# Edge rows of a graph layer: one queue fetches rows singly instead of three engines, and the gathered rows share one pool of eight buffers

## The chip, the cores and the metric

The kernel runs on one core of one Trainium2 chip. The metric is the device time of one execution in microseconds (us); the number quoted for a kernel is the median of its timed runs. The core has five engines with a queue of instructions each: TensorE (PE, with its weight loads shown as PEld), VectorE (DVE), ScalarE (ACT), GpSimd (POOL) and SyncE (SP). They meet only through semaphores, and 16 DMA engines move the data.

## The reference

A graph layer over N = 12500 nodes with 128 features and E = 400000 edges with 32 attributes; the edges come sorted by destination.

```python
h = jnp.maximum(_layernorm(x, axis=-1), 0.0)
# for every edge (s -> d):
m = relu(concat([h[s], h[d], ea]) @ w1 + b1) @ w2 + b2
agg = segment_sum(m, d, num_segments=12500)
# a GRU cell with input agg and state h gives h'
out = x + h'
```

The whole is float32. What costs is `h[s]`: 400000 rows of 512 bytes in random order.

## The kernel before, in words

A first stage normalises all nodes, keeps h transposed on chip (`hT_all`, 128 features by 12500 nodes), multiplies it by the first 128 rows of w1 and writes the product to a table `A` in device memory. After that an edge needs one row of `A` instead of a row of h and a product.

The edges are cut into 391 double groups of 1024 edges (eight tiles of 128; the first has five), numbered k. A double group is two units, u = 2k and 2k + 1, of four tiles each. The loop over u at the end of the kernel writes out the order of all work by hand; for a unit it issues, a few units ahead of each other:

- `pre(u+3)`: TensorE adds destination part and edge attributes into PSUM (L599);
- `add(u+2)`: VectorE adds the gathered rows of `A` in place (L624);
- `relu(u+2)`: ScalarE writes the result to a ring of three `RB` (L630); this is the last reader of the gathered rows;
- `seg(u)`: TensorE sums the edges of a destination with a one-hot matrix (L643), and `take` copies the sums out (L651, L652).

`window`, `onehot` and `onehot_T` prepare the matrices on VectorE. After every 14 double groups `node(b)` runs the GRU for a block of 512 nodes, spread over the units that follow.

The rows of `A` arrive in three ways.

**Gathers.** `gather(k)` issues eight indirect DMAs of 128 rows on GpSimd (L147) into a buffer `G` of 128 x 8 x 128 floats. The buffer is free once the relu of unit 2 x taker + 1 is done, where `taker[k]` is the double group that had it before. The pool `gp` has 7 buffers. Another pool `ge` of 4 buffers serves double groups 0 to 3 and 11 to 14 and is closed at unit 30. The first `RAW` = 10 double groups can't wait for `A`: they gather rows of x, and VectorE, ScalarE and TensorE normalise and turn them on the way (`raw_stats`, `raw_fin`, `raw_h`, `raw_turn`).

**Rows one by one (SyncE).** Six double groups are brought by SyncE: 1024 numbers of source nodes lie in one partition of a small tile `at`; 32 at a time are loaded into registers (L789), and one DMA per row (L802) copies 512 bytes of `A` into a buffer `G_sp` of its own. The queue of SyncE also brings the edge attributes `L` (L486) and the destinations `Ld` (L495) of every second double group, the node numbers (L103, L114), and the rows and results of a node block (L665, L734), in the order in which the loop issues them.

**Columns one by one (VectorE and ScalarE).** For 18 double groups VectorE, and for 19 ScalarE, copies a column of `hT_all` per edge, found by a register, into a tile of 128 x 1024 (L797, L795); `pre` then multiplies these columns by w1 on TensorE (L610), and there is nothing to add.

Which double group goes which way is fixed when the kernel is built (`SPREAD`). `run_jobs` spreads the single copies of a job evenly over the units between its start and its end, four times a unit: a job of SyncE begins two units after the last one's double group and is due 8 units before its own. `gathers(u)` issues each gather as soon as the relu that frees its buffer has been issued.

```python
def gathers(u):
    while asked[0] < NP and (asked[0] in mode or 2 * taker[asked[0]] + 1 < u + 2):
        gather(asked[0])
        asked[0] += 1
```

Of the kernel before, what the change touches and what calls it, by code (L numbers as in the profile page):

```python
# [20 lines left out]

GRP = 4
PAIR = 2 * GRP
SUP0 = T % PAIR
NP = T // PAIR + 1
# [11 lines left out]
NT = -(-N // 128)  # L37
NFULL = N // 128
BAT = (4,) + (8,) * 11 + (NFULL - 92, 1)
RAW = 10  # L40
GBUFS = 7
EARLY = 4
PLACE = 20
CH = PLACE * PAIR
LOAD = 32
STEP = {"act": 4, "dve": 4, "sp": 2}
SPREAD = {"dve": 18, "act": 19, "sp": 6}
NR = 12672

H_AT = 16512  # L50

ROW = 512
HOLD = -2


@with_exitstack
def tile_gnn(ctx: ExitStack, tc: tile.TileContext, x, src, srcT, dstT, dstP, eaT, eaP, w1, b1, w2T, b2,
             wih, bih, whh, bhh, out):
    nc = tc.nc
    ctx.enter_context(tc.manual_schedule())  # L60
    const = ctx.enter_context(tc.tile_pool(name="const", bufs=1))
    hT_all = const.tile([128, N], F32, name="hT_all")
    h_bytes = hT_all.bitcast(U8)
    gp = ctx.enter_context(tc.tile_pool(name="gp", bufs=GBUFS))
    p2 = ctx.enter_context(tc.tile_pool(name="p2", bufs=2))
    p3i = ctx.enter_context(tc.tile_pool(name="p3i", bufs=3))
    early = ExitStack()
    ge = early.enter_context(tc.tile_pool(name="ge", bufs=EARLY, side="right"))
    ps2 = ctx.enter_context(tc.tile_pool(name="ps2", bufs=2, space=bass.MemoryType.PSUM))
    ps1 = ctx.enter_context(tc.tile_pool(name="ps1", bufs=1, space=bass.MemoryType.PSUM))  # L70
    dram = ctx.enter_context(tc.tile_pool(name="dram", bufs=1, space=bass.MemoryType.DRAM))
# [8 lines left out]
        return [(t0 + a * GRP + j, j, a) for j in (2 * h, 2 * h + 1) for a in range(2)  # L80
                if t0 + a * GRP + j < t1]

    JOBS0 = 2 * EARLY + GBUFS

    mode, order = {}, {m: [] for m in SPREAD}
    for m, n in SPREAD.items():
        lo, hi = {"dve": (JOBS0 + 3, NP - 14), "act": (JOBS0 + 11, NP - 6),
                  "sp": (JOBS0 + 5, NP - 10)}[m]
        for i in range(n):
            k = lo + int((i + 1) * (hi - lo) / n)  # L90
            while k in mode:
                k += 1
            mode[k] = m
            order[m].append(k)


    src_i = {}
# [26 lines left out]

    G = {}

    def early_pair(k):
        return k < EARLY or EARLY + GBUFS <= k < 2 * EARLY + GBUFS

    taker, rings = {}, {True: [], False: []}  # L130
    for k in range(NP):
        if k not in mode:
            ring = rings[early_pair(k)]
            size = EARLY if early_pair(k) else GBUFS
            taker[k] = ring[-size] if len(ring) >= size else -1
            ring.append(k)

    def gather(k):
        if k >= NP or k in mode:
            return  # L140
        pool = ge if early_pair(k) else gp
        G[k] = pool.tile([128, GRP, 2, D], F32, name="G")
        table = x if k < RAW else A
        for u in (2 * k, 2 * k + 1):
            for t, j, a in unit_tiles(u):
                c, i = divmod(t, CH)
                nc.gpsimd.indirect_dma_start(  # L147
                    out=G[k][:, j, a, :], out_offset=None, in_=table,
                    in_offset=bass.IndirectOffsetOnAxis(ap=src_i[c][:, i:i + 1], axis=0))
# [61 lines left out]
    with tc.tile_pool(name="pp", bufs=3) as pp:  # L211
# [50 lines left out]
        rows = const.tile([1, 6 * D + D], F32, name="rows")  # L262
# [212 lines left out]


    Ls, Ds, OH, RT, HE, SEG = ({} for _ in range(6))
    hand = {}

    def fetch(q):  # L480
        if q * QP >= NP:
# [109 lines left out]
    def pre(u):  # L591
        if u >= NU:
            return
        k, h = divmod(u, 2)
        PP[u] = ps2.tile([128, GRP, D], F32, name="pre")
        for i in range(2):
            c0 = (k % QP) * 512 + (2 * h + i) * 128
            raw = u in HE or k in hand
            nc.tensor.matmul(PP[u][:, 2 * i:2 * i + 2, :], Ls[k // QP][:, c0:c0 + 128], RW[k % 4],  # L599
                             start=True, stop=not raw)  # L600
            if raw:
                l = unit_tiles(u)
                for n, (t, j, a) in enumerate(l):
                    if j % 2 == i:
                        if k in hand:
                            c = (a * GRP + j) * 128
                            cols = hand[k][:, c:c + 128]
                        else:
                            cols = HE[u][:, n * 128:(n + 1) * 128]
                        nc.tensor.matmul(PP[u][:, 2 * i + a, :], cols, w1a, start=False,  # L610
                                         stop=n + 1 == len(l) or l[n + 1][1] != j)


    def add(u):
        if u >= NU:
            return
        if u in HE or u // 2 in hand:
            RT[u] = PP.pop(u)
            HE.pop(u, None)
            if u % 2:  # L620
                hand.pop(u // 2, None)
        else:
            RT[u] = unit(u)
            nc.vector.tensor_tensor(RT[u], PP.pop(u), RT[u], op=ALU.add)  # L624
# [132 lines left out]
        return o  # L757


    pj = []  # L760
    late = ExitStack()
    by_hand = [k for m in ("sp", "act", "dve") for k in order[m]]
    NJ = len(by_hand)
    NSP = len(order["sp"])

    place_of = const.tile([NJ, 2], F32, name="place_of")
    for i, (to_sp, to_others) in enumerate(((ROW, 4), (0, H_AT))):
        nc.vector.memset(place_of[:, i:i + 1], float(to_others))
        nc.vector.memset(place_of[:NSP, i:i + 1], float(to_sp))
    A_bytes = A.bitcast(U8).rearrange("n f -> (n f)")  # L770
    at = const.tile([NJ, PAIR * 128], I32, name="at")

# [2 lines left out]
        nc.sync.dma_start(at[r:r + 1, :], src[t0 * 128:(t0 + PAIR) * 128].rearrange(  # L775
            "(o e) -> o e", o=1))

    def one_by_one(m, k):
        et = {"act": ET.Activation, "dve": ET.DVE, "sp": ET.SP}[m]
        r = by_hand.index(k)  # L780
        if m == "sp":
            G[k] = pj[0].tile([128, GRP, 2, D], F32, name="G_sp", bufs=1)
            rows = G[k].bitcast(U8)
        else:
            hand[k] = pj[0].tile([128, PAIR * 128], F32, name=f"HE_{m}")
            he = hand[k].bitcast(U8)
        for e0 in range(0, PAIR * 128, LOAD):
            low, high = (0, ROW * (N - 1)) if m == "sp" else (H_AT, H_AT + 4 * (N - 1))
            _, vals = nc.values_load_multi_w_load_instructions(  # L789
                at[r:r + 1, e0:e0 + LOAD], engines=[et], min_val=low, max_val=high,  # L790
                skip_runtime_bounds_check_because="src holds numbers of nodes")
            for i, v in enumerate(vals):
                e = e0 + i
                if m == "act":
                    nc.scalar.copy(he[:, e * 4:e * 4 + 4], h_bytes[:, bass.ds(v - H_AT, 4)])  # L795
                elif m == "dve":
                    nc.vector.tensor_reduce(he[:, e * 4:e * 4 + 4],  # L797
                                            h_bytes[:, bass.ds(v - H_AT, 4), None],
                                            AX.X, ALU.max)
                else:  # L800
                    a, j = divmod(e // 128, GRP)
                    nc.sync.dma_start(rows[e % 128:e % 128 + 1, j, a, :],  # L802
                                      A_bytes[bass.ds(v, ROW)].rearrange("(o f) -> o f", o=1))
                if i % STEP[m] == STEP[m] - 1:
                    yield


    jobs = {}
    for m, kl in order.items():
        start = 2 * JOBS0  # L810
        for k in kl:
            end = 2 * k - (8 if m == "sp" else 4)
            jobs.setdefault(start, []).append((m, k, end - start))
            start = end if m != "sp" else 2 * k + 2
    live = {}

    PH = 4

    def run_jobs(u, phase):
        if u == 2 * JOBS0 and phase == 0:  # L820
            early.close()
            pj.append(late.enter_context(tc.tile_pool(name="pj", bufs=2, side="right")))
        if phase == 0:
            for m, k, span in jobs.get(u, ()):
                live[m] = [one_by_one(m, k), u, span, PAIR * 128 // STEP[m], 0]
        for m, job in list(live.items()):
            it, start, span, steps, done = job
            want = -(-steps * ((u - start) * PH + phase + 1) // (span * PH))
            while job[4] < want:
                job[4] += 1  # L830
                if next(it, "end") == "end":
                    del live[m]
                    break


    asked = [RAW]

    def gathers(u):
        while asked[0] < NP and (asked[0] in mode or 2 * taker[asked[0]] + 1 < u + 2):
            gather(asked[0])  # L840
            asked[0] += 1

# [46 lines left out]
    for u in range(NU):  # L889
        k, h = divmod(u, 2)  # L890
        gathers(u)
        if h == 0:
# [9 lines left out]
                dst_tile(k // PLACE + 2)  # L902
            if k == NP - 20:
                check_windows()
        for r in range(2 * u, min(2 * u + 2, NJ)):
            job_indices(r)
        if u == 2 * JOBS0 - 2:
            nc.vector.tensor_scalar(at, at, place_of[:, 0:1], place_of[:, 1:2],
                                    op0=ALU.mult, op1=ALU.add)

        def other(phase):
            run_jobs(u, phase)
# [190 lines left out]
```

## Time and profile before

| what | before |
|---|---|
| median of 3 runs | 5420.59 us (5406.4 to 5431.38) |
| profiled execution | 5395.6 us, its span 5393.5 us |
| instructions | 95106 |
| busy share PE, DVE, ACT, POOL | 58%, 50%, 50%, 49% |
| gathers of rows of `A` (L147) | 2704, 955 ns each |
| column copies, ScalarE (L795) | 19456, 189 ns each |
| column copies, VectorE (L797) | 18432, 146 ns each |
| row DMAs of SyncE (L802) | 6144 of 0.5 KB |

The profile is one execution. A line of a view names the line of the kernel, the engine, the operation, what it writes and reads, and how often; "idle before" is the time for which the engine had nothing running just ahead of these instructions, and the name after the arrow is what ended most of it ("issue": nothing that the profile shows). Instructions that only load registers, branch or start a DMA are not counted as busy. Times within the run are us from its first instruction.

### The profile page before, as it was taken

What the parts mean: (1) busy time and instruction counts of PE and PEld (TensorE: products, weight loads), DVE (VectorE), ACT (ScalarE), POOL (GpSimd) and SP (SyncE); (2) the same over time, 40 slices, a digit from 0 to 9 for tenths busy, and PEclk for the clock granted to TensorE, in tenths of its full rate; (3) what the DMA queues carried; (4) which work ended last, traced back from release to release, by engine and by line L of the source; (5) the groups of instructions that cost most, each with busy time, mean ns of one, the idle gap of its engine ahead of it and who ended that gap; (6) DMA issues with size and microseconds to landing.
All of it is one profiled execution on the core that took longest, in us unless ns stands there. A gap on an engine that the chain in (4) does not pass through costs nothing. (4 is left out here: it accounts for less than half of the span.)

```text
span 5393.5 us, 95106 instructions
## 1 busy us (share of the span) xinstructions
PE 3101.8 (58%) x13578; PEld 1854.8 (34%) x13578; DVE 2712.7 (50%) x22515; ACT 2718.9 (50%) x20936; POOL 2654.9 (49%) x2789
## 2 busy tenths in 40 slices
PE   2664555556555556556655555665556565556557
PEld 2542333333333323333333333333333233333334
DVE  3645545545454545455545455545454555555453
ACT  2433345555555555555555555555555555555554
POOL 5445445544555454545454555544455544544452
PEclk7775665666566666666666666666666666666667
DMA  3322122222222222222221222222222222222221
GB/s 107 90 65 63 52 58 63 62 56 56 60 59 59 60 60 55 61 57 62 56 60 52 58 61 58 61 60 56 60 58 56 59 60 58 60 58 58 57 58 44
DMA packets 157887, 325.93 MB, mean 60 GB/s; under 512 B 65057, under 2 KB 77132, under 8 KB 157255
## 3 DMA queue, kind: packets, MB, share of 16 engines
q0 software_dynamic: 88992, 182.43, 13.1%
q1 hardware_dynamic: 68119, 137.33, 8.9%
q14 instruction: 520, 4.26, 0.3%
q8 instruction: 112, 1.84, 0.1%
q10 hardware_dynamic: 144, 0.07, 0.0%
HBM read 305.74 MB, written 13.84 MB: 59 GB/s over the span
## 5 line engine op out<-in xcount | busy, mean ns | idle before, releaser
L147 POOL DMA_INDIRECT G<-A,src_i x2704 | 2581.1, 955 | 2658.2 <-ACT RB L630 1766.9
L795 ACT COPY HE_act<-hT_all 128x4 uint8 x19456 | 2155.6, 189 | 1758.6 <-issue 1733.5
L797 DVE TENSOR_REDUCE HE_dve<-hT_all 128x4 uint8 x18432 | 1406.9, 146 | 1166.2 <-issue 1157.3
L599 PE MATMUL pre<-RW,L 128*128 128x256 f32 x3128 | 1369.6, 577 | 901.4 <-DVE G L624 748.7
L599 PEld LDWEIGHTS pre<-RW,L 128*128 128x128 f32 x3128 | 799.3, 282 | 1279.6 <-issue 651.5
L524 PE MATMUL oh<-w1b,hw 128*64 128x128 f32 x782 | 245.4, 412 | 1203.9 <-DVE hw L521 599.5
L643 PE MATMUL seg<-RB,OH 128*32 128x129 f32 x6250 | 716.4, 371 | 0.8 <-issue 0.8
L630 ACT ACTIVATE RB<-G 128x512 f32<-128x512 f32 x676 | 424.8, 629 | 430.9 <-issue 175.0
L533 DVE TENSOR_TENSOR RW<-oh,b1b 32x128 f32<-32x128 f32 x782 | 218.6, 279 | 773.5 <-issue 657.3
L624 DVE TENSOR_TENSOR G<-pre,G 128x512 f32<-128x512 f32 x676 | 460.9, 682 | 276.9 <-issue 269.0
L524 PEld LDWEIGHTS oh<-w1b,hw 128*64 128x64 f32 x782 | 103.6, 188 | 1416.5 <-DVE hw L521 705.7
L643 PEld LDWEIGHTS seg<-RB,OH 128*32 128x32 f32 x6250 | 382.6, 141 | 281.1 <-issue 184.8
L651 DVE COPY sums<-seg 64x128 f32<-64x128 f32 x391 | 107.4, 275 | 181.6 <-remote 94.6
L502 DVE TENSOR_SCALAR L<-Ld,node_of 64x512 f32<-64x512 int32 x391 | 192.3, 492 | 2.1 <-issue 1.6
L652 ACT CAST dcol<-seg 64x1 f16<-64x1 f32 x391 | 59.4, 152 | 232.4 <-DVE sums L651 146.0
L551 DVE TENSOR_TENSOR OH<-dloc,iota 128x256 f32<-128x256 f16 (+1 forms) x392 | 163.0, 416 | 15.2 <-issue 11.7
L674 PEld LDWEIGHTS nd<-spot,sums 64*128 64x128 f32 x782 | 160.6, 314 | 15.5 <-issue 15.5
L674 PE MATMUL nd<-spot,sums 64*128 64x40 f32 x782 | 164.6, 398 | 2.2 <-issue 2.2
L638 PE MATMUL seg<-zrow 1*64 1x129 bf16 x391 | 115.0, 294 | 0.0
L327 PE MATMUL pre<-w1a,hT_all 128*128 128x128 f32 x196 | 51.6, 414 | 77.2 <-remote 30.4
L693 PE MATMUL nd<-DEG,brow 33*128 33x512 f32 x112 | 89.4, 889 | 2.7 <-ACT RB L630 1.7
L697 PE MATMUL nd<-TOT,w2ih 128*128 128x512 f32 x112 | 87.8, 878 | 0.0
(151 smaller groups left out, 1625.5 us busy)
## 6 DMA issues: line engine op xcount, KB each, us to landing
G_sp<-A SPq DMA_DIRECT2D x6144, 0.5 KB
Ld<-in_dstP SPq DMA_DIRECT2D x390, 128.0 KB
L<-in_eaP SPq DMA_DIRECT2D x195, 256.0 KB
G<-A,src_i POOLq DMA_INDIRECT x2704
xb<-in_x SPq DMA_DIRECT2D x28, 256.0 KB
out<-xb SPq DMA_DIRECT2D x28, 256.0 KB
xs<-in_x SPq DMA_DIRECT2D x11, 512.0 KB
A<-asb SPq DMA_DIRECT2D x11, 512.0 KB
```

The lines of the kernel that those rows point to most:

```text
L147: nc.gpsimd.indirect_dma_start(out=G[k][:, j, a, :], out_offset=None, in_=table, in_offset=bass.IndirectOffsetOnAxis(ap=src_i[c][:, i:i + ...
L502: nc.vector.tensor_scalar(Ls[k // QP][:2 * V, c], Ds[k // QP][:, c], node_of[:, k:k + 1], None, op0=ALU.is_equal)
L524: nc.tensor.matmul(PB_[k][:2 * V, :D], hw.rearrange("p a v -> p (a v)"), w1b, start=True, stop=True)
L533: nc.vector.tensor_tensor(RW[k % 4][s, a, :], pm[s, :D], b1b[s, :], op=ALU.add)
L551: nc.vector.tensor_tensor(o, d.to_broadcast(shape), i.to_broadcast(shape), op=ALU.is_equal)
L599: nc.tensor.matmul(PP[u][:, 2 * i:2 * i + 2, :], Ls[k // QP][:, c0:c0 + 128], RW[k % 4], start=True, stop=not raw)
L624: nc.vector.tensor_tensor(RT[u], PP.pop(u), RT[u], op=ALU.add)
L630: nc.scalar.activation(o[:, :, :D], RT.pop(u), AF.Relu)
L643: nc.tensor.matmul(SEG[k][V * a:V * (a + 1), :D + 1], OH[k][:, j, a, :], RB[u % 3][:, (j % 2) * 2 + a, :D + 1], start=False, stop=all(b != ...
L674: nc.tensor.matmul(pt[:, bass.ds(offs[i], V + SHIFT)], sums[:, i, :], spot, start=False, stop=i == n - 1)
L795: nc.scalar.copy(he[:, e * 4:e * 4 + 4], h_bytes[:, bass.ds(v - H_AT, 4)])
L797: nc.vector.tensor_reduce(he[:, e * 4:e * 4 + 4], h_bytes[:, bass.ds(v - H_AT, 4), None], AX.X, ALU.max)
```

## The change

Columns are no longer copied. VectorE's and ScalarE's 37 double groups go back to gathers, with one exception: SyncE fetches the rows of seven double groups instead of six, numbers 70, 122, 174, 225, 277, 329 and 381 (before 80, 140, 200, 260, 320 and 381). With the columns go their register loads on both engines, the multiplication of columns in `pre`, and the table `place_of`, by which node numbers were turned into addresses. `at` has 7 rows of numbers instead of 43, and one multiplication by 512. A job's first unit is 28 instead of 30. Gathered rows have one pool of 8 buffers for the whole run instead of 7 + 4 at first and 7 later, and 8 double groups instead of 10 gather rows of x. The buffer of SyncE's rows is open from the start.

```diff
-RAW = 10
-GBUFS = 7
-EARLY = 4
+RAW = 8
+GBUFS = 8
...
-STEP = {"act": 4, "dve": 4, "sp": 2}
-SPREAD = {"dve": 18, "act": 19, "sp": 6}
+STEP = 2
+SP_PAIRS = 7
...
-    JOBS0 = 2 * EARLY + GBUFS
-
-    mode, order = {}, {m: [] for m in SPREAD}
...
+    JOBS0 = 14
+
+    by_hand = [JOBS0 + 5 + int((i + 1) * (NP - 15 - JOBS0) / SP_PAIRS) for i in range(SP_PAIRS)]
...
-    taker, rings = {}, {True: [], False: []}
+    taker, ring = {}, []
     for k in range(NP):
-        if k not in mode:
-            ring = rings[early_pair(k)]
-            size = EARLY if early_pair(k) else GBUFS
-            taker[k] = ring[-size] if len(ring) >= size else -1
+        if k not in by_hand:
+            taker[k] = ring[-GBUFS] if len(ring) >= GBUFS else -1
             ring.append(k)
...
     def gather(k):
-        if k >= NP or k in mode:
+        if k >= NP or k in by_hand:
             return
-        pool = ge if early_pair(k) else gp
-        G[k] = pool.tile([128, GRP, 2, D], F32, name="G")
+        G[k] = gp.tile([128, GRP, 2, D], F32, name="G")
...
-            raw = u in HE or k in hand
+            raw = u in HE
...
-                        if k in hand:
-                            c = (a * GRP + j) * 128
-                            cols = hand[k][:, c:c + 128]
-                        else:
-                            cols = HE[u][:, n * 128:(n + 1) * 128]
+                        cols = HE[u][:, n * 128:(n + 1) * 128]
...
-        if u in HE or u // 2 in hand:
+        if u in HE:
             RT[u] = PP.pop(u)
...
-    def one_by_one(m, k):
...
+    def one_by_one(r):
+        k = by_hand[r]
+        G[k] = pj.tile([128, GRP, 2, D], F32, name="G_sp")
+        rows = G[k].bitcast(U8)
         for e0 in range(0, PAIR * 128, LOAD):
...
-                if m == "act":
-                    nc.scalar.copy(he[:, e * 4:e * 4 + 4], h_bytes[:, bass.ds(v - H_AT, 4)])
-                elif m == "dve":
-                    nc.vector.tensor_reduce(he[:, e * 4:e * 4 + 4],
-                                            h_bytes[:, bass.ds(v - H_AT, 4), None],
-                                            AX.X, ALU.max)
-                else:
-                    a, j = divmod(e // 128, GRP)
-                    nc.sync.dma_start(rows[e % 128:e % 128 + 1, j, a, :],
-                                      A_bytes[bass.ds(v, ROW)].rearrange("(o f) -> o f", o=1))
+                a, j = divmod(e // 128, GRP)
+                nc.sync.dma_start(rows[e % 128:e % 128 + 1, j, a, :],
+                                  A_bytes[bass.ds(v, ROW)].rearrange("(o f) -> o f", o=1))
...
+            for r, k in enumerate(by_hand):
+                begin = 2 * by_hand[r - 1] + 2 if r else 2 * JOBS0
+                if u == begin:
+                    live[:] = [one_by_one(r), u, 2 * k - 8 - begin, 0]
...
-            nc.vector.tensor_scalar(at, at, place_of[:, 0:1], place_of[:, 1:2],
-                                    op0=ALU.mult, op1=ALU.add)
+            nc.vector.tensor_scalar(at, at, float(ROW), None, op0=ALU.mult)
```

More of the change, by code (lines that the diff above doesn't have):

```diff
@@ L45 @@
 LOAD = 32
-STEP = {"act": 4, "dve": 4, "sp": 2}
-SPREAD = {"dve": 18, "act": 19, "sp": 6}
+STEP = 2
+SP_PAIRS = 7
 NR = 12672
-H_AT = 16512
 ROW = 512
-HOLD = -2
 @with_exitstack
@@ L62, in tile_gnn @@
     hT_all = const.tile([128, N], F32, name="hT_all")
-    h_bytes = hT_all.bitcast(U8)
     gp = ctx.enter_context(tc.tile_pool(name="gp", bufs=GBUFS))
@@ L66, in tile_gnn @@
     p3i = ctx.enter_context(tc.tile_pool(name="p3i", bufs=3))
-    early = ExitStack()
-    ge = early.enter_context(tc.tile_pool(name="ge", bufs=EARLY, side="right"))
     ps2 = ctx.enter_context(tc.tile_pool(name="ps2", bufs=2, space=bass.MemoryType.PSUM))
@@ L81, in unit_tiles @@
                 if t0 + a * GRP + j < t1]
-    JOBS0 = 2 * EARLY + GBUFS
-    mode, order = {}, {m: [] for m in SPREAD}
[L86 to L94, printed above, removed]
+    JOBS0 = 14
+    by_hand = [JOBS0 + 5 + int((i + 1) * (NP - 15 - JOBS0) / SP_PAIRS) for i in range(SP_PAIRS)]
     src_i = {}
@@ L125, in tile_gnn @@
     G = {}
-    def early_pair(k):
-        return k < EARLY or EARLY + GBUFS <= k < 2 * EARLY + GBUFS
-    taker, rings = {}, {True: [], False: []}
+    taker, ring = {}, []
     for k in range(NP):
-        if k not in mode:
-            ring = rings[early_pair(k)]
-            size = EARLY if early_pair(k) else GBUFS
-            taker[k] = ring[-size] if len(ring) >= size else -1
+        if k not in by_hand:
+            taker[k] = ring[-GBUFS] if len(ring) >= GBUFS else -1
             ring.append(k)
     def gather(k):
-        if k >= NP or k in mode:
+        if k >= NP or k in by_hand:
             return
-        pool = ge if early_pair(k) else gp
-        G[k] = pool.tile([128, GRP, 2, D], F32, name="G")
+        G[k] = gp.tile([128, GRP, 2, D], F32, name="G")
         table = x if k < RAW else A
@@ L477, in tile_gnn @@
     Ls, Ds, OH, RT, HE, SEG = ({} for _ in range(6))
-    hand = {}
     def fetch(q):
@@ L616, in add @@
             return
-        if u in HE or u // 2 in hand:
+        if u in HE:
             RT[u] = PP.pop(u)
             HE.pop(u, None)
-            if u % 2:
-                hand.pop(u // 2, None)
         else:
@@ L757, in gates @@
         return o
-    pj = []
     late = ExitStack()
-    by_hand = [k for m in ("sp", "act", "dve") for k in order[m]]
+    pj = late.enter_context(tc.tile_pool(name="pj", bufs=1, side="right"))
     NJ = len(by_hand)
[L764 to L769, printed above, removed]
     A_bytes = A.bitcast(U8).rearrange("n f -> (n f)")
@@ L776, in job_indices @@
             "(o e) -> o e", o=1))
-    def one_by_one(m, k):
[L779 to L783, printed above, removed]
-        else:
-            hand[k] = pj[0].tile([128, PAIR * 128], F32, name=f"HE_{m}")
-            he = hand[k].bitcast(U8)
+    def one_by_one(r):
+        k = by_hand[r]
+        G[k] = pj.tile([128, GRP, 2, D], F32, name="G_sp")
+        rows = G[k].bitcast(U8)
         for e0 in range(0, PAIR * 128, LOAD):
-            low, high = (0, ROW * (N - 1)) if m == "sp" else (H_AT, H_AT + 4 * (N - 1))
             _, vals = nc.values_load_multi_w_load_instructions(
-                at[r:r + 1, e0:e0 + LOAD], engines=[et], min_val=low, max_val=high,
+                at[r:r + 1, e0:e0 + LOAD], engines=[ET.SP], min_val=0, max_val=ROW * (N - 1),
                 skip_runtime_bounds_check_because="src holds numbers of nodes")
@@ L793, in one_by_one @@
                 e = e0 + i
-                if m == "act":
-                    nc.scalar.copy(he[:, e * 4:e * 4 + 4], h_bytes[:, bass.ds(v - H_AT, 4)])
-                elif m == "dve":
-                    nc.vector.tensor_reduce(he[:, e * 4:e * 4 + 4],
-                                            h_bytes[:, bass.ds(v - H_AT, 4), None],
-                                            AX.X, ALU.max)
-                else:
-                    a, j = divmod(e // 128, GRP)
-                    nc.sync.dma_start(rows[e % 128:e % 128 + 1, j, a, :],
-                                      A_bytes[bass.ds(v, ROW)].rearrange("(o f) -> o f", o=1))
@@ L804, in one_by_one @@
-                if i % STEP[m] == STEP[m] - 1:
-                    yield
[L808 to L815, printed above, removed]
+                a, j = divmod(e // 128, GRP)
+                nc.sync.dma_start(rows[e % 128:e % 128 + 1, j, a, :],
+                                  A_bytes[bass.ds(v, ROW)].rearrange("(o f) -> o f", o=1))
@@ L817, in tile_gnn @@
+                if i % STEP == STEP - 1:
+                    yield
     PH = 4
+    live = []
     def run_jobs(u, phase):
-        if u == 2 * JOBS0 and phase == 0:
-            early.close()
-            pj.append(late.enter_context(tc.tile_pool(name="pj", bufs=2, side="right")))
         if phase == 0:
[L824 to L830, printed above, removed]
+            for r, k in enumerate(by_hand):
+                begin = 2 * by_hand[r - 1] + 2 if r else 2 * JOBS0
+                if u == begin:
+                    live[:] = [one_by_one(r), u, 2 * k - 8 - begin, 0]
+        if live:
+            it, begin, span, _ = live
+            want = -(-(PAIR * 128 // STEP) * ((u - begin) * PH + phase + 1) // (span * PH))
+            while live and live[3] < want:
+                live[3] += 1
@@ L831, in run_jobs @@
                 if next(it, "end") == "end":
-                    del live[m]
-                    break
+                    live.clear()
     asked = [RAW]
     def gathers(u):
-        while asked[0] < NP and (asked[0] in mode or 2 * taker[asked[0]] + 1 < u + 2):
+        while asked[0] < NP and (asked[0] in by_hand or 2 * taker[asked[0]] + 1 < u + 2):
             gather(asked[0])
@@ L904, in tile_gnn @@
                 check_windows()
-        for r in range(2 * u, min(2 * u + 2, NJ)):
+        for r in range(u, min(u + 1, NJ)):
             job_indices(r)
         if u == 2 * JOBS0 - 2:
-            nc.vector.tensor_scalar(at, at, place_of[:, 0:1], place_of[:, 1:2],
-                                    op0=ALU.mult, op1=ALU.add)
+            nc.vector.tensor_scalar(at, at, float(ROW), None, op0=ALU.mult)
         def other(phase):
```

## The prediction

> **What bounds the kernel now.** I read the page first: no engine is busy for more than 58%, so the bound is a rhythm, not an engine. The groups (instructions by line) show who waits.
>
> ```profile
> PE 3101.8 (58%) x13578; PEld 1854.8 (34%) x13578; DVE 2712.7 (50%) x22515; ACT 2718.9 (50%) x20936; POOL 2654.9 (49%) x2789
> ...
> L147 POOL DMA_INDIRECT G<-A,src_i x2704 | 2581.1, 955 | 2658.2 <-ACT RB L630 1766.9
> L795 ACT COPY HE_act<-hT_all 128x4 uint8 x19456 | 2155.6, 189 | 1758.6 <-issue 1733.5
> L797 DVE TENSOR_REDUCE HE_dve<-hT_all 128x4 uint8 x18432 | 1406.9, 146 | 1166.2 <-issue 1157.3
> ```
>
> GpSimd idles as long as it gathers, and it idles for the relu that frees a buffer. Next, the timeline of GpSimd (start, us, line, idle before):
>
> ```profile
> 2119.32 0.94 POOL L147 DMA_INDIRECT G<-A,src_i  x1 [0.30 <-issue]
> 2123.87 1.53 POOL L147 DMA_INDIRECT G<-A,src_i  x1 [3.61 <-ACT RB L630]
> ...
> 2138.12 0.94 POOL L147 DMA_INDIRECT G<-A,src_i  x1 [3.83 <-ACT RB L630]
> ```
>
> Eight gathers take 8 x 1.249 = 10.0 us start to start, then comes a gap of 4 us, again and again, although seven buffers stand between. From the starts of the gathers and the ends of the relus: a burst of eight begins 0.27 us after the relu that frees its buffer. 286 cycles in which the consumer passes no double group done singly take 14.18 us on average; 38 with one take 24.0.
>
> Why is the relu always late? Windows (length, busy us and instructions per engine) of one burst at 241.56, before any column is copied, show it:
>
> ```profile
> 241.60:249.60 8.00, 7.87 (x51) 6.52 (x51) 6.13 (x35) 3.87 (x11) 6.17 (x7) 0.81 0.18 47
> 249.60:252.90 3.30, 0.00 (x0) 0.00 (x0) 0.00 (x0) 1.14 (x3) 1.32 (x2) 0.78 0.18 46
> ```
>
> For 8 us everything runs; then the other engines stand until just after the burst's last row has landed. Over the nine bursts of this stretch (193 to 300 us) the core starts 16 to 21 instructions a us in the first eight us, 4 to 5 from the ninth to the twelfth. With columns the drop comes from the fifth us (23 down to 6). In a long burst it is plainer. The gathers of x run without a gap until 99 us:
>
> ```profile
> 89.37 0.18 DVE L184 BATCH_NORM_AGGREGATE mv<-bn 128x2 f32<-128x6 f32 x1 [0.41 <-issue]
> 90.77 0.18 DVE L184 BATCH_NORM_AGGREGATE mv<-bn 128x2 f32<-128x6 f32 x1 [1.22 <-DVE mv L184]
> 92.18 0.18 DVE L184 BATCH_NORM_AGGREGATE mv<-bn 128x2 f32<-128x6 f32 x1 [1.23 <-DVE mv L184]
> ...
> 115.55 0.63 DVE L184 BATCH_NORM_AGGREGATE mv<-bn 128x2 f32<-128x6 f32 x8
> ```
>
> One 0.18 us instruction per 1.4 us during it, eight in 0.63 us after 111 us. So gathers that are not slowed themselves slow all others, the more the longer they run without a pause and the more instructions there are. I call this the slow phase. It ends 1.5 us after a burst of 8, and 12 us after the 77. What it is, the trace doesn't say. SyncE's rows obey it too:
>
> ```profile
> 2050.95 6.48 SPq L802 DMA_DIRECT2D G_sp<-A  x20
> ...
> 2142.74 22.97 SPq L802 DMA_DIRECT2D G_sp<-A  x36
> ```
>
> 0.32 us a row undisturbed, 0.6 and more otherwise; the mean between rows with no register load between is 0.59 us.
>
> **The change part by part.** *Columns.* 19456 x 189 ns and 608 register loads of 1.99 us leave ScalarE (its 1.21 ms of loads is most of its "issue"), 18432 x 146 ns and 576 loads of 2.12 us leave VectorE. None of it counts as such: the rhythm is the path. What counts is how a cycle shrinks. A least-squares line through the 286 cycles gives 10.8 us + 0.0174 per column copy (103 in a mean cycle, 1.8 us) + 0.09 per row DMA of SyncE (18, 1.6 us). With no columns and 20 rows a double group (7 x 1024 over 367): 10.8 + 1.8 = 12.6 us. Beside it stands the measured stretch without columns or rows, 12.1 us, its consumer heavier by the normalisation of x. Ends: 10.0 (gathers alone) and 14.2 (as now). I take 12.6, nearest to 12.1, with 11.4 to 13.4 for its own spread.
>
> *Double groups.* 338 gather from A now, 376 after. A cycle with a double group done singly costs 9.8 us more (24.0 - 14.2); an undisturbed consumer needs 4.6 us a double group (relus at 327.18 to 341.02 us: six units in 13.84). Seven remain, 7 us each (ends 4.6 and 9.8): 49 us.
>
> *Start.* 61 gathers of x instead of 77 end at 79 us instead of 99, and the slow phase behind them shrinks from 12 to about 9.5 us: the first stage should gain 22 us (ends 0 and 25). Against it, 8 buffers instead of 11: the first gather from A waits for the first x double group to be turned (193 us now, 171 then), where now it starts at 167.7. Eight x double groups at 12.1 us: double group 15 starts at 256, 16 at 268 us.
>
> *End.* The last gather ends 54.8 us before the end now; the ring is full then as after (8 instead of 7): 57 us.
>
> *Small.* 592 products with columns (L610, 0.27 to 0.34 us) leave TensorE and 74 additions (L624, 0.68 us) come to VectorE: nothing, in the 8 us of a cycle that run freely; without that cover 50 us. The index loads on SyncE's queue fall from 43 to 7 (0.25 us each, done by 305 us): nothing, hidden by the x stage. The table's memsets: nothing.
>
> *SyncE.* A seventh job adds 1024 row DMAs, 1024 register moves and 32 register loads (2.12 us) to its queue, and jobs have 46.8 double groups each instead of some 55, of shorter cycles. A late row DMA delays the `Ld` and `L` loads queued behind it, and `onehot_T` and `pre` wait for those; they are issued three double groups ahead. Where SyncE is early it waits for `L` (289 us in 52 waits now), which then ends at the same relu rhythm. At 0.34 us a row a job takes 348 + 68 + 50 (23 `Ld`/`L` loads of 1.4 us, node blocks) = 466 us of the 590 that 46.8 cycles offer: hidden. At today's 0.59 it is 722 us: not hidden.
>
> Sum: 268 + 367 x 12.6 + 9.7 + 49 + 57 = 5008 us of span, 5010 of execution. The profiled execution stands 0.46% under the median of the runs (5395.6 to 5420.6), so 5033; I say 5030, 7% less.
>
> Against the page "SBUF — State Buffer" of the Trainium skill, section "Who interferes with whom": it says that DMA never contends with a compute engine, save that VectorE in some modes starves descriptor making on GpSimd, that tensor_reduce never does so, and that ScalarE and TensorE wait for nobody. By that page columns and gathers can't disturb each other, the cycle stays at 14.2 us, and the sum is 268 + 367 x 14.2 + 116 = 5595 us: slower. The rows above disagree: gathers keep 938 to 944 ns, and the others stop.
>
> A second rule speaks against the seventh job. "DMA: Bandwidth & Descriptors", sections "Anatomy of one DMA" and "Rules for kernel authors", puts some 2 us fixed cost on a DMA and asks to coalesce small ones: 7168 rows, one behind the other, would be an estimated 14 ms. The trace shows 0.32 us from row to row, so they overlap.
>
> **The rivals.** *GpSimd becomes the bound.* If without columns the slow phase never stops the consumer, bursts join: 10.1 us a cycle, 268 + 367 x 10.1 + 10 + 38 = 4023, 4040 by the median. For it: 4.6 us a double group undisturbed. Against: the gathers of x, unbroken, stopped everything.
>
> *SyncE becomes the bound (slower).* If rows keep 0.59 us, seven jobs of 722 us follow one another: first job at 250 us, 7 x 722, fourteen double groups (176) and the end (57): 5537, 5560 by the median. Place: the queue of SyncE, L802 ahead of L495 and L486. For it: the mean of now. Against: rows issued with gathers running but few columns in the last 8 us keep 0.26 to 0.34 us. It decides from 0.57 us a row, where the sum reaches 5395.
>
> *The cycle does not shrink.* If columns have no share in it, 14.2 us as in the sum above: 5595, 5620. For it: the regression's terms are not causes by themselves. Against: the 12.1 us.
>
> **How the numbers follow.** The cycle shrinks to 11.4 to 13.4 us: 0.70 (4570 to 5300 of execution, 4590 to 5325). GpSimd bound: 0.08. SyncE bound: 0.14. No shrinking: 0.08. Half a per cent, 27 us, is about what a measurement of this kernel can tell. Faster: 0.70 + 0.08, less 0.01 for cycles close to 13.7: 0.77. Same: 0.03, the gap between the first case and SyncE's. Slower: 0.20. The range leaves out GpSimd's case below and the last one above: 4480 to 5570.
>
> **What would show it.** Right: the idle time of L147 still ends at ACT RB L630; bursts start every 12 to 13 us; the drop in instructions comes at the eighth us of a burst; rows of L802 at 0.3 to 0.45 us; no column lines; about 58000 instructions. Wrong: gathers without gaps (first rival); waits of `onehot_T` (L502) or `pre` (L599) for Ld, L or G_sp, and gaps that end later (second); a cycle of 14 us with no columns in it (third). The prediction fails most easily if SyncE's 44 instructions a double group lengthen the slow phase as columns do.

## The result, and the profile after

| | before | after |
|---|---|---|
| median | 5420.5 us | 5575.11 us (5562.81 to 5592.95) |
| ratio | | 1.0294, 95% interval 1.026 to 1.0328 |
| span of the profiled execution | 5393.5 us | 5561.0 us |
| instructions | 95106 | 57483 |
| bursts of gathers | 330 of eight, 4 of sixteen | 71 of eight, 151 of sixteen, 1 of 24 |
| time per double group, relu 16 to relu 388 | 13.44 us | 13.82 us |

The change made the kernel 2.9% slower; 7% faster was forecast. The number is that of the rival "SyncE becomes the bound" (5560), which had 0.14. The granted clock of TensorE rose, from 0.654 to 0.674 in the profiled executions, so a lower clock is not the reason. In the changed kernel the gather is L125, `pre` L576, the addition L595, the relu L601, the row DMAs L753, `L` L463, `Ld` L472 and the register load L747. From the page and its groups (count | busy us, mean ns | idle before, what ended it):

```profile
PE 2693.6 (48%) x12938; PEld 1588.2 (29%) x12938; DVE 1494.3 (27%) x4097; ACT 678.7 (12%) x1460; POOL 2932.6 (53%) x3077
...
L125 POOL DMA_INDIRECT G<-A,src_i x3008 | 2873.8, 955 | 2550.7 <-ACT RB L601 1269.7
L576 PE MATMUL pre<-RW,L 128*128 128x256 f32 x3128 | 1231.4, 530 | 1820.1 <-DMA L<-in_eaP 1467.5
```

ScalarE fell from 50% to 12%, VectorE from 50% to 27%, and yet the gathers idle almost as long as before. New is who is late: `pre` waits for `L`, the edge attributes that SyncE's queue brings. The waits of the engines (us in total, times, longest) say it per wait, first TensorE's after, then SyncE's own before and after:

```profile
PE pre L576 <- DMA L<-in_eaP: 1467.5, 118, 24.8
```

```profile
SPq L495 <- DVE L L502: 289.4, 52, 24.8
```

```profile
SPq L472 <- DVE L L479: 157.3, 9, 33.3
```

Twelve us a time, 118 times, with 196 loads of `L`; the kernel before has this wait not once. SyncE itself hardly waits for anyone: by its instructions' starts, its waits ahead of `Ld` and `L` between 343 and 5473 us sum to 85 us, against 493 us before (343 to 5300 us); the 157.3 us of the line above lie outside that stretch. It is the engine that never rests. Of those 5130 us the 7168 rows take 4253 (0.593 us each, their register moves included), the 224 register loads 404 (1.81 us), the `Ld` and `L` loads about 350, their waits included. The seven jobs take 706 to 757 us each and follow one another within 8 to 21 us.

Why does a row still cost 0.59 us? The timeline of GpSimd (start, us, idle before) shows two double groups in one burst, of which these are the first and last gathers and the neighbours:

```profile
2009.36 0.95 POOL L125 DMA_INDIRECT G<-A,src_i  x1 [0.30 <-issue]
2013.99 0.95 POOL L125 DMA_INDIRECT G<-A,src_i  x1 [3.68 <-ACT dcol L623]
...
2032.76 0.95 POOL L125 DMA_INDIRECT G<-A,src_i  x1 [0.30 <-issue]
2037.65 0.95 POOL L125 DMA_INDIRECT G<-A,src_i  x1 [3.94 <-ACT RB L601]
```

The windows of this burst (length, busy us and instructions of PE, PEld, DVE, ACT, POOL, then granted clock, busy share of the DMA engines and GB/s):

```profile
2014.00:2022.00 8.00, 5.43 (x27) 3.21 (x27) 2.25 (x6) 1.26 (x2) 6.17 (x7) 0.79 0.18 45
2022.00:2036.00 14.00, 1.94 (x11) 0.96 (x11) 3.06 (x8) 0.79 (x2) 8.96 (x10) 0.50 0.20 51
2036.00:2040.00 4.00, 0.00 (x0) 0.00 (x0) 0.00 (x0) 0.63 (x1) 1.89 (x2) 0.50 0.07 18
```

Eight free microseconds, as in a burst of eight before, and then not three but fourteen us in which PE starts 11 matmuls. SyncE's rows in the same three windows: 16, 8 and 10. Over 149 bursts of sixteen (28.2 us from one to the next) SyncE starts 1.9 rows a us in the first six us, 0.8 from the sixth to the 22nd, and 2.3 after that. SyncE's timeline shows the loads of `L` 35 us apart, 42 rows between them:

```profile
2005.94 0.70 SPq L463 DMA_DIRECT2D L<-in_eaP  x1
2008.73 30.72 SPq L753 DMA_DIRECT2D G_sp<-A  x42
...
2041.13 0.49 SPq L463 DMA_DIRECT2D L<-in_eaP  x1
```

One `L` serves two double groups: TensorE waits for it, works off both and frees two buffers. This fits bursts of sixteen, but it is not their only reason: they stay in the runs below in which TensorE never waits for `L`. Why bursts join is not shown further than that.

### The profile page after: what moved, and what is told of

It is laid out like the page before. It is cut to its first block, busy times and chain, and to the rows that moved or that the text cites. A ratio compares the mean times of both kernels' runs of the same rounds, so it can differ in the third digit from the quotient of the medians.

```text
span 5561.0 us, 57483 instructions
## 1 busy us (share of the span) xinstructions
PE 2693.6 (48%) x12938; PEld 1588.2 (29%) x12938; DVE 1494.3 (27%) x4097; ACT 678.7 (12%) x1460; POOL 2932.6 (53%) x3077
## 5 line engine op out<-in xcount | busy, mean ns | idle before, releaser
L125 POOL DMA_INDIRECT G<-A,src_i x3008 | 2873.8, 955 | 2550.7 <-ACT RB L601 1269.7
L576 PE MATMUL pre<-RW,L 128*128 128x256 f32 x3128 | 1231.4, 530 | 1820.1 <-DMA L<-in_eaP 1467.5
L576 PEld LDWEIGHTS pre<-RW,L 128*128 128x128 f32 x3128 | 740.6, 260 | 2178.7 <-issue 2025.8
L601 ACT ACTIVATE RB<-G 128x512 f32<-128x512 f32 x752 | 474.3, 631 | 1746.3 <-DVE G L595 844.7
L614 PE MATMUL seg<-RB,OH 128*32 128x129 f32 x6250 | 642.4, 340 | 3.5 <-issue 3.5
L501 PE MATMUL oh<-w1b,hw 128*64 128x128 f32 x782 | 204.4, 351 | 749.8 <-DVE hw L498 537.7
L595 DVE TENSOR_TENSOR G<-pre,G 128x512 f32<-128x512 f32 x752 | 514.1, 684 | 11.2 <-PE pre L576 0.3
L650 PE MATMUL misc<-spot_h,dcol 128*128 128x40 f16 x391 | 37.5, 200 | 153.2 <-issue 153.2
L498 DVE COPY hw<-hT_all 128x64 f32 x391 | 86.0, 220 | 17.4 <-DVE G L595 9.3
L664 PE MATMUL misc<-DEG,brow 33*128 33x512 f32 x112 | 77.5, 778 | 0.1
```

Of the source, the lines that this page charges most:

```text
L125: nc.gpsimd.indirect_dma_start(out=G[k][:, j, a, :], out_offset=None, in_=table, in_offset=bass.IndirectOffsetOnAxis(ap=src_i[c][:, i:i + ...
L501: nc.tensor.matmul(PB_[k][:2 * V, :D], hw.rearrange("p a v -> p (a v)"), w1b, start=True, stop=True)
L601: nc.scalar.activation(o[:, :, :D], RT.pop(u), AF.Relu)
L614: nc.tensor.matmul(SEG[k][V * a:V * (a + 1), :D + 1], OH[k][:, j, a, :], RB[u % 3][:, (j % 2) * 2 + a, :D + 1], start=False, stop=all(b != ...
```

## The experiments

Theory 1: the changed kernel is bound by SyncE's queue, whose rows the slow phase holds at 0.59 us. Theory 2: the cycle of the consumers stays at 14 us without columns, and SyncE is busy only because nobody asks it to be quicker. To theory 1 belong two questions: is it the number of DMAs, and what keeps a row at 0.59 us?

One thing has to be known to read the numbers. The runs landed on four chips, and on two of them the slow phase is absent: there the kernel before takes 3649 and 3644 us. On the other two it takes 5497 to 5519 us, with the rhythm of the recorded profiles (5420 us). I call them chips without and with the slow phase. Only the latter speak about this result, and each run is compared with the kernel before on its own chip.

### The changed kernel and the kernel before again

No edit.

> The changed kernel unaltered. The four kernels of the first call ran on a chip on which the kernel before takes 3649 us instead of 5420, with gathers in one unbroken chain and rows at 0.32 us from row to row while gathers run. Theory 1 (the slow phase behind the gathers belongs to a chip or its condition, and SyncE's queue is the bound where it is present): where the kernel before takes some 5420 us, 5575 us and a row at 0.5 to 0.6 us; where it takes some 3650, 3008 gathers x 1.255 + 200 = 3975 us at the least, that is slower by 9% or more than the kernel before on the same chip, because 302 gathers more are on GpSimd, the bound there. Theory 2 (the first call's gain came from taking rows off SyncE, not from the chip): about 5575 us also where the kernel before takes 3650.

> The changed kernel unaltered, on the same chip as the three others of this call, to be compared with them directly. Where the kernel before takes some 5450 us: 1.03 of it, about 5620 us. Where it takes some 3650: theory 1 (a row at 0.32 to 0.36 us there, so seven jobs of some 600 us fit) 3008 x 1.255 + 200 = 3975 us; rival (the stalls of the run with the loads on ScalarE show that rows behind the node blocks' loads bound it even there) 4400 us.

> The kernel before unaltered, for its profile on the same chip. Where it takes some 3650 us, theory 1 expects no slow phase: gathers joined with hardly a gap (2704 x 1.25 = 3380 us of 3650), other engines starting instructions at one rate throughout. Where it takes some 5420 us: bursts of eight every 14.2 us, as recorded.

Measured, with the slow phase: 5664.26 us, ratio 1.0314 (1.0281 to 1.0346), and 5714.03 us, 1.0357 (1.0339 to 1.0374): the result repeats. The kernel before, 5493.67 us, shows 334 bursts of eight and two of sixteen, and jobs of 749 to 846 us. The changed kernel was not run on a chip without the slow phase.

### Four jobs instead of seven

```diff
-SP_PAIRS = 7
+SP_PAIRS = 4
```

> Four double groups by SyncE instead of seven, the same kernel as the run with four jobs. On a chip where the kernel before takes some 5420 us: theory 1 (SyncE's queue is the bound of the changed kernel) 4850 to 5050 us (cycles of 12.1 to 12.6); theory 2 (a cycle of 14 us whatever SyncE does) 5560 us. On a chip where it takes some 3650 us: 3980 us as in the first call.

> SyncE fetches four double groups instead of seven; the other three go back to gathers. Theory 1 (SyncE's queue is the bound of the changed kernel: 7168 rows at 0.59 us, with the loads of L and Ld behind them): SyncE needs about 4 x 715 = 2900 us for its jobs and has slack; the cycle falls to the 12.1 to 12.6 us of the prediction: 268 + 371 x 12.3 + 4 x 7 + 67 = 4930 us, 4850 to 5050. Theory 2 (the consumer's cycle stays at 14 us without columns, SyncE is busy only because it is never asked to be faster): 268 + 371 x 14 + 95 = 5560 us, no change.

With the slow phase 5090.15 us, ratio 0.9277 (0.9236 to 0.9318): 10% less than the changed kernel on the same chip, by taking three double groups off SyncE's queue and giving GpSimd 24 gathers more. Theory 2 falls. The largest waits of SyncE's queue in this run:

```profile
SPq L472 <- DVE L L479: 353.8, 57, 38.3
SPq L463 <- PE seg L614: 125.8, 33, 6.2
SPq L753 <- DMA G_sp<-A: 55.8, 104, 1.2
```

SyncE waits for its buffers again, 57 times, and `pre` does not wait for `L` once (118 times in the changed kernel). A double group takes 12.54 us from relu 16 to relu 388. Yet 151 of the bursts are still sixteens, 25.2 us from one to the next: the slow phase has not gone, SyncE is merely early enough.

Without the slow phase the same kernel takes 3981.07 us, 1.092 (1.0897 to 1.0942) of the kernel before. I had expected 4850 to 5050 or 5560 and knew nothing of such chips. What bounds it there stands in the group of the gathers, whose idle time is the 0.30 us between two of them:

```profile
L125 POOL DMA_INDIRECT G<-A,src_i x3032 | 2913.0, 961 | 952.5 <-issue 902.2 <-PE misc L561 28.3 <-DMA G<-A,src_i 12.2
```

### No rows at all

```diff
-SP_PAIRS = 7
+SP_PAIRS = 0
```

(`at` keeps one unused row.)

> SyncE fetches no rows; all double groups after the first eight are gathered from A. Theory 1: no rows in SyncE's queue, cycle 10.8 (intercept of the regression) to 12.1 us (the stretch without rows and columns): 268 + 375 x 10.8 + 57 = 4375 to 268 + 375 x 12.1 + 57 = 4860 us. Theory 2 (cycle of 14 us whatever SyncE does): 268 + 375 x 14 + 57 = 5575 us. Theory 3 (GpSimd bound, bursts joined): 268 + 375 x 10.1 + 57 = 4110 us.

> No rows by SyncE at all. Where the kernel before takes some 5450 us: by the regression of the prediction (0.09 us per row in a cycle) a cycle of 10.8 us, 268 + 375 x 10.8 + 57 = 4375 us, to one of 12.1, 4860 us. Rival (rows cost nothing as long as SyncE is not the bound, the cycle of bursts of 16 is 12.6 us) 268 + 375 x 12.6 + 57 = 5050 us. Where the kernel before takes some 3650: 4025 us as in the first call.

Both landed on chips without the slow phase: 4024.95 us, 1.1037 (1.1019 to 1.1055), and 4023.07 us, 1.104. That is 44 us more than with four jobs, for 32 gathers more at 1.25 us. What it takes with the slow phase was not measured.

### Two rows in one DMA

The same seven double groups, the same bytes and register loads, half the DMAs, and with each DMA its register move, so half of those too (3584 of each instead of 7168). The second row of a pair is not the one that its edge asks for:

```diff
-                nc.sync.dma_start(rows[e % 128:e % 128 + 1, j, a, :],
-                                  A_bytes[bass.ds(v, ROW)].rearrange("(o f) -> o f", o=1))
+                if i % 2 == 0:
+                    nc.sync.dma_start(rows[e % 128:e % 128 + 2, j, a, :],
+                                      A_bytes[bass.ds(v, 2 * ROW)].rearrange("(o f) -> o f", o=2))
```

(`A` has one more row, so that the last one can be followed.)

> Seven jobs, but one DMA of SyncE brings two neighbouring rows of A for every second edge, so 512 instead of 1024 per job, with the same bytes and register loads (the second row of each pair is not the one the edge asks for, so the fetched double groups are computed from wrong rows). Theory 1: a job costs 512 x 0.59 + 67 + about 100 for the other loads = 470 us instead of 715, SyncE has slack, and the cycle is that of the prediction or the one of four jobs: 4850 to 5050 us. Theory 2: no change, 5575 us.

> The kernel of the run with two rows in a DMA: seven jobs, 512 DMAs each. Where the kernel before takes some 5450 us: theory 1 (the number of DMAs in SyncE's queue is the bound of the changed kernel) 512 x 0.59 + 67 + 190 for other loads = 560 us a job, hidden under 52 cycles of 12.6: 4950 to 5100 us, as with four jobs. Theory 2 (the seven double groups themselves, by their bytes or their place in the order, cost the time) 5575 us or more. Where the kernel before takes some 3650: 3953 us as in the first call.

> As for the run with two rows in a DMA before this one, on the chip where it lands. Where the kernel before takes some 5450 us: theory 1 (the number of DMAs in SyncE's queue) 4950 to 5100 us; theory 2 (the seven double groups themselves) 5575 us or more. Where it takes some 3650: 3950 us, as twice before.

With the slow phase 5073.63 us, 0.9187 (0.9156 to 0.9218), and 0.888 of the changed kernel on the same chip. Jobs take 580 to 675 us, `pre` does not wait for `L` once, and SyncE waits again:

```profile
SPq L473 <- DVE L L480: 400.8, 64, 34.2
```

So it is the number of instructions that SyncE has to start for the rows, not the seven double groups, their bytes or their places. Whether the DMAs or their register moves weigh more, the run can't tell, since both were halved. A double group takes 12.56 us, as with four jobs. Without the slow phase: 3953.4 and 3948.29 us, 1.083 and 1.084.

### A pause on GpSimd

Work is added to the changed kernel: ten small memsets after each double group's gathers.

```diff
                     in_offset=bass.IndirectOffsetOnAxis(ap=src_i[c][:, i:i + 1], axis=0))
+        if k >= RAW:
+            for _ in range(10):
+                nc.gpsimd.memset(pause, 0.0)
 
+    pause = const.tile([128, 160], F32, name="pause")
     for k in range(RAW):
```

> The changed kernel with ten small memsets on GpSimd behind the eight gathers of a double group. Where the kernel before takes some 5450 us: theory 1a (rows are slow because bursts join to 16) bursts of eight, rows at 0.4 to 0.45 us, 5080 to 5300 us; theory 1b (rows are slow whatever the burst) 5575 us or more. Where it takes some 3650: 5112 us, as measured there.

> The changed kernel, and GpSimd clears a scratch tile ten times, about 2.7 us, after the eight gathers of each double group: work is added to an engine. Where the kernel before takes some 5450 us: theory 1a (rows take 0.59 us because the gathers of two double groups join to bursts of 16, behind which everything crawls) the bursts stay at eight, a row falls to 0.4 to 0.45 us, SyncE is no longer the bound and the cycle is 12.5 to 13.2: 5080 to 5300 us, faster than the changed kernel by 5 to 9%. Theory 1b (a row takes 0.59 us whatever the length of the bursts) 5575 us, since GpSimd idles for 2550 us and 376 x 2.7 = 1015 us hides there. Where the kernel before takes some 3650: GpSimd is the bound, 3975 + 1015 = 4990 us.

With the slow phase 5190.14 us, 0.9403 (0.9387 to 0.9419): 900 us of useless work make the changed kernel 9% faster (5190.14 / 5714.03 = 0.908). GpSimd's timeline:

```profile
2095.09 1.18 POOL L125 DMA_INDIRECT G<-A,src_i  x1 [0.30 <-issue]
2096.27 2.86 POOL L130 MEMSET pause<- 128x160 f32 x10
2099.62 0.95 POOL L125 DMA_INDIRECT G<-A,src_i  x1 [0.49 <-ACT dcol L627]
...
2109.56 2.85 POOL L130 MEMSET pause<- 128x160 f32 x10
2112.90 0.95 POOL L125 DMA_INDIRECT G<-A,src_i  x1 [0.49 <-issue]
```

No burst is longer than eight; 13.3 us from start to start, with hardly any idle time. GpSimd is the bound now. A row costs 0.50 us (3569 us for 7168) instead of 0.61 in the changed kernel on that chip, a job 606 to 635 us instead of 727 to 774, and SyncE waits for its buffers again:

```profile
SPq L476 <- DVE L L483: 312.3, 28, 25.7
```

Theory 1a holds in its direction and in the time (5080 to 5300 expected); the row is dearer than its 0.40 to 0.45. On a chip without the slow phase the same kernel takes 5111.83 us, 1.5% less than with it, while the kernel before takes a third less: GpSimd, which the slow phase does not slow, bounds the kernel on both. Its rows do feel the slow phase: 0.50 us with it, 0.36 without. Without it the pause costs about what it adds: on that chip the run with two rows in a DMA, which has as many gathers, takes 3948.29 us, 1164 us less, and the 376 pauses last 1081 us.

### Half the pause

The same with five memsets, 1.45 us; then that with four jobs.

> Seven jobs, and five memsets instead of ten. Where the kernel before takes some 5500 us: if half the pause keeps the bursts at eight, rows stay at 0.5 us, SyncE needs 7 x 620 us and the cycle lies between 11.5 (GpSimd) and 12.9 us (as with ten memsets): 4650 to 5190 us. If it is too short, bursts join and SyncE is the bound again: 5400 to 5700 us. Where it takes some 3650: 3975 + 376 x 1.45 = 4520 us.

> Four jobs instead of seven, and five memsets (1.45 us) on GpSimd behind the eight gathers of a double group. Where the kernel before takes some 5500 us: if the joining of bursts is what holds the cycle at 12.6 us with four jobs (25.1 us for a burst of 16 and its gap), the cycle is that of GpSimd, 10.05 + 1.45 = 11.5 us, 260 + 371 x 11.5 + 65 = 4590 us, up to 4850 if the slow phase behind a burst of eight (it ended 1.5 us after the last gather) makes some relus late. If a pause of 1.45 us is too short to empty what makes the others crawl, bursts join again and it stays at 5000 to 5090. Where the kernel before takes some 3650: 3980 + 379 x 1.45 = 4530 us.

Both with the slow phase. Seven jobs: 5150.19 us, 0.9345 (0.9323 to 0.9367), jobs of 646 to 718 us, and TensorE waits for `L` once more, so that SyncE is the bound again, on a lower level, 12.75 us a double group. No burst is longer than eight here either, yet a row costs 0.55 us; the length of the bursts is not all that sets its price, the pause behind them counts too:

```profile
PE pre L580 <- DMA L<-in_eaP: 1163.9, 109, 17.7
```

Four jobs: 4889.24 us, 0.8862 (0.8827 to 0.8896), the fastest version with the slow phase, 11% under the kernel before. A double group takes 12.05 us, not the 11.5 of GpSimd alone: some bursts still wait for a relu (191 us in 65 waits). The expected 4590 to 4850 was missed by 40 us.

### The columns alone

The kernel before, with nothing but its columns taken out:

```diff
-SPREAD = {"dve": 18, "act": 19, "sp": 6}
+SPREAD = {"dve": 0, "act": 0, "sp": 6}
```

> The kernel before without its columns, SyncE's six jobs kept. Where the kernel before takes some 5450 us: theory 1 (columns lengthen the cycle, six jobs fit) 5080 to 5250 us; rival (columns have no share, or six jobs bound it already) 5400 us or more. Where it takes some 3650: 3953 us, as measured there.

> The kernel before with its column copies alone taken out (those 37 double groups are gathered); SyncE's six jobs and the pools of 7 and 4 buffers stay. Where the kernel before takes some 5450 us: theory 1 (columns lengthen the cycle, and six jobs still fit: 6 x 671 us + 375 x 1.2 us of other loads = 4480 us) cycle 12.6 us, 5080 to 5250 us, faster than before by 4 to 7%. Rival (columns have no share in the cycle, or six jobs already bound it) 5400 us or more. Where the kernel before takes some 3650: 37 double groups more on GpSimd, the bound, 3650 + 37 x 10 = 4020 us at most.

With the slow phase 5421.67 us, 0.9829 (0.9812 to 0.9845): 1.7% less, as the rival had it (5400 or more) and not theory 1's 5080 to 5250. The bursts join here too (145 of sixteen), with 7 buffers and ten double groups of x: it is the columns' absence that joins them, not the eight buffers. And six jobs, now 786 to 850 us, bind it already:

```profile
PE pre L599 <- DMA L<-in_eaP: 910.7, 91, 23.1
```

The rest of the change (the seventh job, the one pool of eight buffers, eight double groups of x) takes the kernel from 5421.67 to 5714.03 us on that chip; of these parts only the number of jobs was varied alone, from seven to four.

Without the slow phase: 3952.99 us, 1.0854 (1.0836 to 1.0872).

### The loads of L and Ld from ScalarE's queue

```diff
-        nc.sync.dma_start(Ls[q][2 * V:, :n * 512], eaP[:, c])
+        nc.scalar.dma_start(Ls[q][2 * V:, :n * 512], eaP[:, c])
...
-            nc.sync.dma_start(Ds[q][V * a:V * (a + 1), :n * 512],
+            nc.scalar.dma_start(Ds[q][V * a:V * (a + 1), :n * 512],
```

> Seven jobs as in the changed kernel, the loads of L and Ld issued from ScalarE's queue. Where the kernel before takes some 5500 us: theory 1 (the cost lies in the loads of L behind rows) the waits for L go; rows at 0.55 us make 630 us a job, and the cycle is 12.6: 5050 to 5200 us. Rival (rows themselves, and the node blocks' loads behind them, are late all the same): waits for the rows and for xb take the place, 5500 to 5750 us. Where it takes some 3650: 4431 us as in the first call.

> Seven jobs as in the changed kernel, but the loads of L and Ld are issued from ScalarE's queue, so that no row stands ahead of them. Theory 1, with the place named in the rival (rows ahead of these loads): the consumer waits for SyncE only at the end of a job; rows alone are 7 x (1024 x 0.52 to 0.59 + 67) = 4200 to 4700 us behind a start at 343 us, so 5010 us (cycle of 12.6) to 5130. Theory 2: no change, 5575 us. If the rows themselves are what is late (each job's last row), it stays within 2% of the changed kernel and the wait moves from L to G_sp.

Neither theory had this: 6754.05 us with the slow phase, 1.2259 (1.2232 to 1.2287), and 4431.33 us without, 1.2145. `pre` does not wait for `L` any more. In its place stands the node block, whose load `xb` is still behind the rows:

```profile
DVE xb L703 <- DMA xb<-in_x: 1456.7, 17, 103.6
```

A job grew to 871 to 944 us. In these traces a row waits until the last DMA that used its semaphore has landed. By the semaphores of its instructions, a row stood for over 2 us behind a load in three cases in the changed kernel; here 171 rows stand for 1658 us in all behind an `Ld` load that ScalarE's queue had issued on the same semaphore. Moving the loads thus brought a new loss with it, and the run by itself does not settle where the old one lay. That `L` behind the rows is the place of the loss in the changed kernel rests on the waits of `pre` there, which vanish in the two runs that relieve SyncE (four jobs, two rows in a DMA).

## Why the prediction was wrong, step by step

**SyncE** is the step that failed: "At 0.34 us a row a job takes ... 466 us of the 590 that 46.8 cycles offer: hidden. At today's 0.59 it is 722 us: not hidden." Measured: 0.593 us a row and 706 to 757 us a job. (A late job has the 52 double groups up to the next one, not 46.8; at 12.6 us that is 655 us, still too little.) I took the price from rows issued while gathers run and few columns have just been copied, on the ground that columns had made the others dear. That choice picked something else, the first microseconds of a burst. In the trace before, of the rows issued while gathers run and with fewer than 40 column copies in the 8 us ahead, 166 lie in the first five us of their burst and take 0.36 us each, and the 29 later ones take 1.64 us. So the choice hid how far the burst had run. And the slow part of a cycle did not get smaller: before, it was the fifth to the eleventh us of a cycle of 14; without columns a burst joins the next, and it is some 16 us of 28. The price stayed (0.600 us before, 0.593 after). That the rhythm of the gathers moves the price is shown by the pauses: 0.50 us with ten memsets, 0.55 with five, 0.61 with none on such chips.

The prediction held the right price too, with its result (5560); giving it 0.14 was the misjudgement. That 5560 comes so close is partly luck: the first job starts at 341 us, not 250, the seven jobs take 5132 us, not 5054, and from the last row to the end it is 88 us, not 233. The point named there, 0.57 us a row, is where the sum reaches the time before. SyncE becomes the bound sooner: by the same terms seven jobs reach the forecast 5008 us at an estimated 0.52 us a row, and with five memsets, at 0.55, it was the bound.

**The cycle without columns**: 12.6 us forecast; 12.54 and 12.56 us measured where SyncE is not the bound (four jobs, two rows in a DMA). The size was right and the picture wrong: not bursts of eight every 12.6 us but sixteens every 25.2, so the agreement is luck. The row's term of the regression did not carry over: four jobs and two rows in a DMA have 11 and 10 row DMAs a double group, for which the line gives 11.8 and 11.7 us.

**Start**: the gathers of x end at 79.4 us (79 forecast), the first gather from A starts at 173.5 (171), double group 16 at 279 (268). **End**: from the last gather's end to the end of the span 57.0 us, as forecast. **Small** terms: nothing in the trace contradicts that they are hidden, and no run tests it. The seven singly fetched double groups at 7 us each can't be told apart once SyncE is the bound.

**The other rivals.** GpSimd becomes the bound: not here, yet it is what happens on chips without the slow phase. The cycle does not shrink: 13.82 us looks like it, but the runs with SyncE relieved contradict. The rule of the Trainium skill's page "SBUF — State Buffer", section "Who interferes with whom", by which the span was to be 5595 us, came within 1% of the measured 5561 for a reason that the runs contradict: without columns and with SyncE relieved the cycle is 12.5 us, not 14.2.

**The rule on small DMAs** of the Trainium skill's page "DMA: Bandwidth & Descriptors", section "Rules for kernel authors", which I set aside, was right in direction: halving SyncE's DMAs is worth 11%. The estimate of 14 ms, made from the fixed cost in the section "Anatomy of one DMA", is far off: all rows together took 4.25 ms, at 0.59 us from one to the next. That section gives the cost for DMAs issued on GpSimd, and these come from SyncE's queue.

**The signs.** For the second rival I had named waits of `pre` for `L`, and they are the largest wait for a transfer. "Gaps that end later" are there too. The instruction count (57483 for 58000) and the missing columns were bound to be right. Idle time of the gathers still ends at the relu.

## What to carry to other kernels

A queue whose price per item was measured under one rhythm has another price when the change alters the rhythm: ask what the removed work was holding apart, and price the queue that gets the new work at the rate of today until the trace shows a reason for less. If work is removed and hardly any time goes, look for the engine that has stopped waiting. An engine that runs ahead can cost more than it gains: here a pause of 3 us on GpSimd, in every double group, gained 9% where the slow phase is present, and cost what it added where it is not.

## What the runs showed of the hardware

**The slow phase belongs to the chip or its condition, not to the program.** The same kernel with four jobs took 3981 us on one chip and 5090 on another. VectorE's first stage, while the gathers of x run, shows the difference bare; first without the slow phase (start, us; five instructions in 0.43 us), then with it:

```profile
61.14 0.43 DVE L162 BATCH_NORM_AGGREGATE mv<-bn 128x2 f32<-128x6 f32 x5
```

```profile
61.53 0.18 DVE L162 BATCH_NORM_AGGREGATE mv<-bn 128x2 f32<-128x6 f32 x1 [1.22 <-DVE mv L162]
62.93 0.18 DVE L162 BATCH_NORM_AGGREGATE mv<-bn 128x2 f32<-128x6 f32 x1 [1.22 <-DVE mv L162]
```

The gathers take the same on both (961 and 953 ns). What differs between the chips stays open; no run here shows it. (The granted clock of TensorE in the kernel before was 0.78 to 0.79 without the slow phase and 0.65 to 0.66 with it, as cause or as consequence.) For the change it decides the sense of every edit: with the slow phase, relieving SyncE and pausing GpSimd gain up to 11%; without it, columns that spare gathers are worth 8.5% (3952.99 against 3644 us), and every version run there loses to the kernel before.

**With the bursts kept apart, the slow phase costs the whole kernel little.** With 3 us between bursts of eight, the chip without it takes 1.5% less than the one with it (5111.83 and 5190.14 us); with four jobs and no pause 22% less, in the kernel before a third less. The other engines are still slowed: SyncE's rows take 0.50 us against 0.36.
